# A graph network on one core: layer 2's input product y made by rows, with the data stationary and the weights moving

## The chip, the core and the metric

The kernel runs on one core of a Trainium2 chip. The metric is the device time of one execution in microseconds (us), the median of several runs. A profile of one execution gives the durations below; its times are counted from the start of its span. The engines are TensorE (PE: matmuls, with its weight loads listed apart as PEld), VectorE (DVE), ScalarE (ACT), GpSimd (POOL) and SyncE (SP), which here only issues DMAs. SBUF is the on-chip memory with 128 partitions; PSUM is the memory that TensorE writes its results to.

## The reference

Four graph layers run one after the other on 16 graphs of 1024 nodes with 128 features each; all of it in float32. Between layers the result is added to the input and normalised along the features. Layer 0 is a gated attention, layer 1 three graph convolutions with batch norm, layer 2 an attention with three gates, layer 3 three graph convolutions. The change lies where the end of layer 1 enters layer 2:

```python
h1 = _bn(jax.nn.relu(_sage(x, adj_d, Wr1, Wx1, b1, mf)), g1, be1)
h2 = _bn(jax.nn.relu(_sage(h1, adj_d, Wr2, Wx2, b2, mf)), g2, be2)
h3 = _bn(jax.nn.relu(_sage(h2, adj_d, Wr3, Wx3, b3, mf)), g3, be3)
xc = jnp.concatenate([h1, h2, h3], axis=-1) * mf[..., None]
return (xc @ Wl + bl) * mf[..., None]          # this is y
```

So y (1024 rows of 128 per graph) is the sum of three products of h1, h2, h3 with the three 128x128 blocks of Wl, plus a bias bl along the row, times a mask mf per row. It is then added to x, normalised (mean and variance along the features), and goes into layer 2. A batch below is one of the 16 graphs.

## The kernel before

The kernel has one code path for the general case and a fast one; the profile shows the fast one. Its stages follow each other: layer 0 (to about 740 us), the thinning of the adjacency for layer 1 (to about 1150 us), layer 1 (to about 1825 us), and layers 2 and 3 together (the rest). Each h_l is written to DRAM transposed, as 128 features x 1024 nodes, before batch norm. The batch norm, which is known only when all 16 batches are done, is a scale and an offset per feature (`bn_ab`). `take_norms` (L1220) folds it into layer 2's weights: the scale into the rows of Wl, the offset through a product with Wl into the bias.

Layers 2 and 3 work on one batch at a time in three generators: `before` (L1541: y, the addition to x, layer norm, x transposed, and the products hT and G), `attention` (L1574: eight blocks of 128 rows; each makes scores `pmm` on TensorE, a masked maximum `em` on VectorE at L1587, an exponential on ScalarE at L1591, a scaled `hs` on VectorE at L1598, and a product into `acc` on TensorE at L1601) and `after` (L1604: gates, layer norm, then layer 3: an ELU into `ehi` at L1505 to L1513, products with U at L1522 giving `zn`, `zhi`, `zlo`, and products with the adjacency at L1536). `in_turn` (L814) runs them interleaved: `before` of batches 0 and 1 first, then, for each batch b, `after` of b-1, `attention` of b and `before` of b+1. A scheduler of the framework turns this into one fixed order of instructions for each engine and places the waits. Each engine works through its order one after the other.

In `before`, y is made transposed: for each half of 512 nodes, three products with Wl stationary and hb (the transposed h_l) moving sum in PSUM; ScalarE copies the half into yT and adds the bias, which is a column there; four transposes on TensorE turn it back to rows, and VectorE multiplies them by the mask into yn (L1551). VectorE then adds yn to xn (L1554).

Helpers: `halves` (L747) gives two PSUM tiles of 512 columns, `turned` (L753) transposes eight blocks into them (L758), and `products` (L761) sums products into them (L765). The PSUM pool `ps_h` has two buffers, which all of these share. `normed` (L786) is the layer norm: statistics on VectorE (`ln_st`, `ln_mv`), a power on GpSimd (`ln_rstd`, L744), `ln_nb` on VectorE (L798), and eight ScalarE operations on xn (L800). The inputs of a batch come by SP's queue in `load` (L1229): A8, the three tiles hb0 to hb2 (one buffer each) and xn. `dB` (L1636) is a row of degrees for layer 3 from the same queue.

## Time and profile before

| what | value |
|---|---|
| median of 3 runs | 3009.3 us |
| lowest and highest of them | 3008.72 and 3012.13 us |
| the profiled run, timed | 3009.7 us |
| span of its profile | 3007.9 us |
| mean granted TensorE clock | 0.971 |
| y: products L765 with hb | 192 records, median 592 ns |
| y: transposes L758 of yT | 128 records, median 273 ns |
| y: ScalarE L1548, yT | 32, median 668 ns |
| y: VectorE L1551, yn | 32, median 681 ns |
| addition L1554 to xn, whole | 14, about 1220 ns |

A float32 product shows as two records each for the weight load and the matmul, a transpose as one. Lines of a timeline give the start, the length, the engine, the line, the operation, its output and inputs, their shapes and how many records are merged; a bracket at the end gives idle time of the engine before it and what ended it. The ends of matmuls are modelled, so that merged records overlap the next row; the starts are what to go by. The granted clock is a share of TensorE's full speed.

### The profile page before, as it was taken

How to read it: one execution, taken by the hardware profiler on the slowest of the kernel's cores; microseconds unless marked ns; L12 is line 12 of the kernel's file. 1: busy time of each engine (PE TensorE's matmuls, PEld its weight loads, DVE VectorE, ACT ScalarE, POOL GpSimd, SP SyncE). 2: the span in 40 equal slices, each digit the busy share in tenths (PEclk: the TensorE clock that was granted, in tenths of full speed). 3: DMA queues.
4: the chain of work that ended last, by engine and by line, in shares of the span. 5: the costliest groups of instructions: out<-in, count | busy, mean ns of one | idle time of the engine just before them, and what ended most of it. 6: DMA issues, size and time to landing. Idle time of an engine off the chain costs nothing.

```text
span 3007.9 us, 42998 instructions
## 1 busy us (share of the span) xinstructions
PE 2738.6 (91%) x15219; PEld 1719.6 (57%) x15282; DVE 2329.1 (77%) x5987; ACT 2028.3 (67%) x3475; POOL 324.1 (11%) x295
## 2 busy tenths in 40 slices
PE   7999999996999988999999987999999999999995
PEld 3444444443666566887788874455555555555554
DVE  6898899887999995776688785766777777777765
ACT  5777787774788877665555434766666676676763
POOL 0000000003000001211122231000010001000000
PEclk9999999998999999999999997999999999999998
DMA  4344444431000024223367692011111111111000
GB/s 157 133 161 153 135 140 161 148 126 36 2 2 2 2 102 143 99 99 127 127 234 250 227 342 84 36 56 58 63 69 61 64 70 66 56 57 57 22 15 23
DMA packets 124129, 297.98 MB, mean 99 GB/s; under 512 B 12672, under 2 KB 65664, under 8 KB 116736
## 3 DMA queue, kind: packets, MB, share of 16 engines
q1 hardware_dynamic: 103440, 211.65, 20.8%
q0 software_dynamic: 20464, 83.47, 7.4%
q8 instruction: 123, 2.02, 0.3%
q14 instruction: 102, 0.84, 0.1%
HBM read 211.04 MB, written 84.02 MB: 98 GB/s over the span
## 4 chain that ended last, share of the span: by engine, by line
PE 36%; DVE 23%; issue 21%; ACT 9%; DMA 6%; POOL 5%; SPq 0%; POOLq 0%; DVEq 0%; ACTq 0%
PE ph L1536 8%; PE acc L1293 6%; PE ph L765 5%; PE acc L1601 4%; DMA an<-in_adj 4%; PE pmm L723 3%; POOL ln_rstd L744 3%; DVE ln_st L793 3%; ACT xn L800 3%; PE ph L1397 3%; PE ph L758 3%; PE ph L1522 2%; DVE em L1587 2%; ACT em L969 2%; PE acc L976 2%
## 5 line engine op out<-in xcount | busy, mean ns | idle before, releaser
L723 PE MATMUL pmm<-G,hT 128*128 128x512 f32 x1024 | 505.9, 611 | 7.7 <-DVE mx L1587 7.2
L800 ACT ACTIVATE xn<-xn,ln_nb,ln_rstd 128x128 f32<-128x128 f32 x512 | 207.6, 481 | 115.2 <-DVE ln_nb L798 115.2
L723 PEld LDWEIGHTS pmm<-G,hT 128*128 128x128 f32 x1024 | 178.5, 193 | 175.5 <-issue 139.9
L976 PE MATMUL acc<-em,hs 128*128 128x512 f32 x512 | 243.3, 598 | 16.7 <-DVE hs L973 15.2
L1293 PE MATMUL acc<-a,lo 128*128 128x512 f32 x768 | 243.0, 400 | 15.2 <-DVE lo L1260 15.2
L744 POOL TENSOR_TENSOR ln_rstd<-ln_rstd,mhalf 128x8 f32<-128x8 f32 (+1 forms) x68 | 113.6, 1671 | 1329.1 <-DVE ln_rstd L741 608.8
L1601 PE MATMUL acc<-em,hs 128*128 128x512 f32 x512 | 249.3, 606 | 3.6 <-DVE hs L1598 1.9
L1293 PE MATMUL acc<-a,hi 128*128 128x512 f32 x768 | 244.1, 402 | 3.7 <-ACT hi L1259 3.5
L1140 ACT ACTIVATE q<-s,negc 128x512 f16<-128x512 f32 x256 | 170.5, 697 | 57.9 <-DVE negc L1119 22.3
L922 ACT ACTIVATE ab<-an 128x1024 bf16<-128x1024 f32 x128 | 134.5, 1052 | 105.9 <-DMA an<-in_adj 75.6
L1138 PE MATMUL s<-step,carry 128*128 128x384 bf16 (+3 forms) x1034 | 197.8, 302 | 7.5 <-DVE carry L1108 3.2
L1152 ACT ACTIVATE carry<-pc,negone 128x512 fp8e4<-128x512 f32 x256 | 166.8, 699 | 36.6 <-PE pc L1151 27.2
L965 DVE CUSTOM_DVE_ANT_0 em<-pmm,msk 128x1024 f32<-128x1024 f32 x128 | 155.9, 1218 | 30.0 <-PE acc L976 26.3
L1587 DVE CUSTOM_DVE_ANT_0 em<-pmm,msk 128x1024 f32<-128x1024 f32 x128 | 155.7, 1216 | 25.5 <-PE acc L1601 20.9
L1293 PEld LDWEIGHTS acc<-a,lo 128*128 128x128 f32 x768 | 143.9, 189 | 54.6 <-DVE lo L1260 21.2
L925 DVE SCALAR_TENSOR_TENSOR chk<-an 128x1024 fp8e4<-128x1024 f32 x128 | 156.4, 1222 | 14.8 <-DMA an<-in_adj 14.1
L1293 PEld LDWEIGHTS acc<-a,hi 128*128 128x128 f32 x768 | 142.9, 190 | 37.1 <-ACT hi L1259 4.0
L1582 ACT ACTIVATE msk<-A,nbig 128x1024 bf16<-128x1024 fp8e4 x128 | 145.8, 1140 | 26.7 <-DVE mx L1587 23.4
L930 DVE TENSOR_SCALAR carry<-pt 128x1024 fp8e4<-128x1024 bf16 x128 | 155.6, 1216 | 6.5 <-PE pt L929 6.5
L1397 PE MATMUL ph<-Wx,hT 128*128 128x128 f32 x768 | 152.3, 281 | 5.0 <-DVE l2WT L709 3.2
L969 ACT ACTIVATE em<-em,nmx 128x1024 f32<-128x1024 f32 x128 | 146.8, 1147 | 12.3 <-DVE nmx L967 11.9
L976 PEld LDWEIGHTS acc<-em,hs 128*128 128x128 f32 x512 | 90.7, 190 | 112.1 <-issue 86.8
(289 smaller groups left out, 6258.9 us busy)
## 6 DMA issues: line engine op xcount, KB each, us to landing
an<-in_adj SPq DMA_DIRECT2D x128, 512.0 KB, 4.1
adj_d<-carry POOLq DMA_DIRECT2D x16, 1024.0 KB, 4.9
A<-dil_d SPq DMA_DIRECT2D x16, 1024.0 KB, 6.8
rdeg<-rdeg_d SPq DMA_DIRECT2D x32, 512.0 KB, 4.3
ag_d<-ag POOLq DMA_DIRECT2D x32, 512.0 KB, 5.3
ag<-ag_d SPq DMA_DIRECT2D x32, 512.0 KB, 6.0
A<-adj_d SPq DMA_DIRECT2D x16, 1024.0 KB, 4.7
xn<-in_x SPq DMA_DIRECT2D x16, 512.0 KB, 4.0
```

The source lines that it names most:

```text
L723: nc.tensor.matmul(p[:, h * 512:(h + 1) * 512], lhsT, rhs[:, h * 512:(h + 1) * 512], start=True, stop=True)
L744: nc.gpsimd.tensor_tensor(r, r, mhalf[:, :n], op=OP.pow)
L800: nc.scalar.activation(r[:, k.start + i, :], r[:, k.start + i, :], AF.Identity, scale=rstd[:, i:i + 1], bias=nb[:, i:i + 1])
L969: nc.scalar.activation(em, em, AF.Exp, bias=nmx, accum_out=sm)
L976: nc.tensor.matmul(s.acc[:, c], hs, em[:, c], start=(jt == 0), stop=(jt == NT - 1))
L1138: nc.tensor.matmul(s[:, lo or 0:], y, twos if lo is None else step[:, :512 - lo], start=(j == 0), stop=(j == len(terms) - 1))
L1140: nc.scalar.activation(q[:, h * 512:(h + 1) * 512], s, AF.Abs, bias=st.negc[:, i:i + 1])
L1293: nc.tensor.matmul(acc, part[:, jt, :], pieces[h * NT // 2 + i][:, j, :], start=(jt == 0 and p == 0), stop=(jt == NT - 1 and p == 1))
L1397: nc.tensor.matmul(p[:, i * P:(i + 1) * P], x[:, j * P:(j + 1) * P], W, start=(n == 0), stop=(n == 1))
L1536: nc.tensor.matmul(p, part[:, jt, :], A[:, jt, c], start=(jt == 0 and i == 0), stop=(jt == NT - 1 and i == 1))
L1587: nc.vector.tensor_tensor_reduce(em, e, msk, 1.0, 0.0, op0=OP.add, op1=OP.max, accum_out=mx)
L1601: nc.tensor.matmul(s.acc[:, c], hs, em[:, c], start=(jt == 0), stop=(jt == NT - 1))
```

## The change

y is made by rows. For each of four blocks of 128 nodes in a half, the block of hb is the stationary operand and Wl moves: three products of 128 columns sum to 128 rows of y in PSUM. This makes 24 products a batch instead of 6, and no transposes and no yT. The bias is now a row, the same on all partitions (`blrow`), and VectorE adds it on the way out of PSUM; a second VectorE operation multiplies by the mask in place. `take_norms` makes the offset as a row too: the offset column of `bn_ab`, repeated 128 times, is stationary, and Wl moves.

```diff
-            self.blcol = column(wts, t["L1_gnn_bl"], "blcol")
+            self.blrow = row_bcast(wts, t["L1_gnn_bl"], P, "blrow")
...
-            pc = psum.tile([P, 1], F32, name="pc", tag="h")
+            pc = psum.tile([P, P], F32, name="pc", tag="h")
             for l in range(3):
-                nc.tensor.matmul(pc, self.Wl[:, l, :], bn_ab[l][:, 1:2], start=(l == 0), stop=(l == 2))
-            nc.vector.tensor_add(self.blcol, self.blcol, pc)
+                nc.tensor.matmul(pc, bn_ab[l][:, 1:2].to_broadcast([P, P]), self.Wl[:, l, :], start=(l == 0), stop=(l == 2))
+            nc.vector.tensor_add(self.blrow, self.blrow, pc)
...
-            yT = wide("yT")
-            for p, c in products(ps_h, *((Wl[:, l, :], s.hb[l]) for l in range(3))):
-                nc.scalar.activation(yT[:, c], p, AF.Identity, bias=blcol)
             yn = rows("yn", 2)
-            for p, c, k in turned(ps_h, yT):
-                nc.vector.tensor_mul(yn[:, k, :], tiles3(p), half_rows(mf[:, b * NT + k.start:b * NT + k.stop]))
+            for p, c, blocks in halves(ps_h):
+                for i, j in enumerate(blocks):
+                    for l in range(3):
+                        nc.tensor.matmul(p[:, i * P:(i + 1) * P], s.hb[l][:, j * P:(j + 1) * P], Wl[:, l, :],
+                                         start=(l == 0), stop=(l == 2))
+                k = slice(blocks[0], blocks[-1] + 1)
+                y = yn[:, k, :]
+                nc.vector.tensor_add(y, tiles3(p), blrow[:, None, :].to_broadcast([P, 4, P]))
+                nc.vector.tensor_mul(y, y, half_rows(mf[:, b * NT + k.start:b * NT + k.stop]))
```

Lines after the change are shifted: the new products are L1550, the addition L1554, the multiplication L1555, the addition to xn L1558; later lines are four higher.

## The prediction

> **What bounds the kernel now.** I read the page's busy shares first, then the two windows of the last stage that differ, then the order of instructions around the lines that change. The page says that no engine is idle enough to be ignored:
>
> ```profile
> PE 2738.6 (91%) x15219; PEld 1719.6 (57%) x15282; DVE 2329.1 (77%) x5987; ACT 2028.3 (67%) x3475; POOL 324.1 (11%) x295
> ```
>
> The change touches only the stage after 1828 us: a start-up of two batches (1828 to 1854 us), then one period per batch. The y products of batches 2 to 15 begin at 1903.73, 1974.81, 2046.41, 2117.43, 2188.04 ... 2825.20 us: 14 times, (2825.20 - 1903.73)/13 = 70.9 us apart. In the table by windows (PE, PEld, DVE, ACT, POOL, clock, DMA) TensorE is busy 92 to 97% there, VectorE 66 to 76%:
>
> ```profile
> 2000.00:2100.00 100.00, 93.08 (x366) 58.49 (x367) 66.66 (x194) 63.75 (x125) 6.83 (x4) 0.97 0.12 43
> 2200.00:2300.00 100.00, 91.89 (x341) 53.61 (x339) 72.71 (x234) 69.18 (x139) 10.11 (x6) 0.97 0.13 44
> ```
>
> Busy time alone would say "TensorE". The timelines of one period say more (start, length, then what ended the idle time in brackets):
>
> ```profile
> 2046.41 3.60 PE L765 MATMUL ph<-hb,Wl 128*128 128x512 f32 x8
> 2049.84 3.60 PE L1601 MATMUL acc<-em,hs 128*128 128x512 f32 x8
> 2053.27 1.88 PE L765 MATMUL ph<-hb,Wl 128*128 128x512 f32 x4
> 2054.99 0.60 PE L758 MATMUL ph<-identf,yT 128*128 128x128 f32 x4
> 2055.43 1.88 PE L1601 MATMUL acc<-em,hs 128*128 128x512 f32 x4
> 2057.15 0.60 PE L758 MATMUL ph<-identf,yT 128*128 128x128 f32 x4
> 2063.38 1.87 PE L758 MATMUL ph<-identf,xn 128*128 128x128 f32 x5 [2.20 <-ACT xn L800]
> ```
> ```profile
> 2051.76 1.23 DVE L1587 CUSTOM_DVE_ANT_0 em<-pmm,msk 128x1024 f32<-128x1024 f32 x1 [1.58 <-PE acc L1601]
> 2056.38 0.69 DVE L1551 TENSOR_TENSOR yn<-ph,mf 128x512 f32<-128x512 f32 x1
> 2062.63 0.17 DVE L798 SCALAR_TENSOR_TENSOR ln_nb<-ln_mv,ln_rstd 128x8 f32<-128x8 f32 x1 [1.55 <-POOL ln_rstd L744]
> ```
>
> The y work lies in the one part of the period where TensorE does idle: 2.20 us before the transposes of xn, and 2.01 us at 2073.00 (waiting for ehi). In that part the chain of waits runs on VectorE: em after the acc products, gating, layer norm, ELU. VectorE itself waits 1.58 us just before em. So a saving on TensorE counts only as far as it brings that em forward, or as other products move into the gaps.
>
> [...] the duration of a 128x128 f32 record (275 ns) is not its price. The timeline of L1397, the same form as the new products (data stationary, a weight matrix moving), shows the pace:
>
> ```profile
> 1600.94 0.39 PE L1397 MATMUL ph<-Wx,hT 128*128 128x128 f32 x2
> 1603.62 0.39 PE L1397 MATMUL ph<-Wx,hT 128*128 128x128 f32 x2
> ```
>
> Twelve products of two records in 2.68 us: 0.223 us a product, weight load included. [...] Here the granted clock was 0.50 from 1828 to 1834 us. [...] the power on GpSimd takes 2.62 us at 2059.98, beside the xn addition L1554, and 1.64 us at 2065.35. [...] the trace's 128x512 subtraction L1527 takes 686.
>
> **The change, part by part.** Removed per batch: six products of 128x512 (12 records at 3.43/8 = 0.43 us: 5.16 us), eight transposes (4 take 0.44 us: 0.88 us), two ScalarE evictions yT (0.668 us each). Added: 24 products at 0.223 us = 5.36 us (from above, 0.128 us a record, the pace that L1522's 16 records in 2.05 us show: 6.14), and two VectorE operations. VectorE before: two multiplications from PSUM, 0.68 us each. After: two additions from PSUM with a broadcast row (L1399, the same form, median 0.682 us) and two multiplications SBUF to SBUF (0.69 us). So TensorE -0.68 us (bound: +0.10), ScalarE -1.34, VectorE +1.37 per batch.
>
> Where that lies follows from the built order of the changed kernel, laid against the timeline above, with the start of the y products as zero. TensorE: 14 products (3.13), four acc products (3.44), ten products (2.23), two acc products (1.72): 10.5 us against 11.2 before. VectorE gets the first half's addition and multiplication between the hs scalings, before em. The first half is ready at 12 x 0.223 = 2.7 us, when VectorE comes free (about 3.0), so these two (1.3 us) fall into the 1.58 us in which it waited: no cost. Em can start 3.13 + 1.72 = 4.85 us after zero instead of 5.16: -0.31. The second half's addition and multiplication stand where the two old multiplications stood: no change. Its addition may wait up to 0.4 us for the second half (8.8 us); queued behind it are layer-norm statistics of the batch before, for which TensorE's xn transposes wait. Two further moves: one acc product (0.86 us) now lies between L1522 and L1536, where TensorE idled 0.44 us, so 0.42 net is gained; and y starts up to 0.46 us earlier, after half a product pmm instead of a whole one. Both bounds of one period: nothing gained if the VectorE chain decides, 0.31 + 0.42 + 0.46 = 1.2 us if all add up. I take 0.6, close to the saved TensorE time: 14 x 0.6 = 8.4 us.
>
> Start-up. The tiles hb0 to hb2 have one buffer, so batch 1's loads wait until batch 0's products have read them. Before, each layer's tile was free after its own two products:
>
> ```profile
> 1830.29 0.32 SPq L1235 DMA_DIRECT2D hb<-h0T_d  x1
> 1830.71 0.38 SPq L1636 DMA_DIRECT2D dB<-dinv_d  x1
> 1833.71 0.32 SPq L1235 DMA_DIRECT2D hb<-h1T_d  x1
> 1834.87 0.32 SPq L1235 DMA_DIRECT2D hb<-h2T_d  x1
> ```
> ```profile
> 1837.39 4.56 PE L765 MATMUL ph<-hb,Wl 128*128 128x512 f32 x10 [0.20 <-DVE yn L1551]
> 1843.72 1.64 PE L758 MATMUL ph<-identf,yT 128*128 128x128 f32 x8 [1.77 <-ACT yT L1548]
> ```
>
> After, the last block of rows reads all three. Two products run earlier; 22 remain from 1828.3: 25 of the 44 records at half clock (0.223 us) until 1834, 19 at 0.112: end 1836.1. The three loads are issued at about 1835.9, 1836.3 and 1836.7; with the 4.8 us to landing that this window's table of DMA issues gives for h2T, the third is there at 1841.5. TensorE idles 5.3 us, so I expect half clock for 3 to 6 us, and an end of the 24 products at 1848.3 to 1850. Add three VectorE operations (2.0): 1850.3 to 1852, against 1847.28 for the last xn addition before. The transposes and the products L765 of both batches stand behind this on TensorE. I take +4 us (from +1.2 at full clock to +5). The wait moves dB ahead of hb on SP's queue; dB waits for work finished by 1828, so nothing stands behind it.
>
> One-off terms: blrow's load is 64 KB written instead of 0.5 KB, with over 80 us to land; three products of 128 columns instead of one for the offset and an addition of 0.28 instead of 0.15 us, on the path: +0.2. Batch 0's hb2 load moves behind two loads on SP, some 5 us, with 36 us to spare. Sum: -8.4 + 4 = -4.4 (the 0.2 is in the 1828.3). Against the profiled span 3007.9 that gives 3003.5; that run was timed at 3009.7 and the median is 3009.3, so I carry the difference over: 3009.3 - 4.4 = 3004.9.
>
> **The rivals.**
> - *TensorE bounds all the way*: the whole 0.68 to 1.0 us per period is gained and the start-up costs 1.2: about -10 us, 2999. For it: TensorE 94% busy, and periods of different VectorE order before are within 1.1 us of each other (70.48 to 71.60). Against: TensorE's waits from 1850 to 2950 us sum to 70.6 us, 4.5 per period.
> - *The period is set by the VectorE chain*: the first half comes too late for the gap or the gap closes, but nothing is lost. Steady gain 0, start-up +4: 3013. For it: y lies wholly in the part with idle TensorE.
> - *VectorE becomes the bound*: the 1.37 us stand in its queue ahead of em and the statistics. It decides from the point at which VectorE comes to the first addition with under 1.3 us left before em. 14 x 1.37 + 4 = +23: 3032; a third of it, 3015.7, is already slower. For it: em and ln_st hold 5.9% and 5.4% of the chain of waits from 1850 to 2950 us. Against: the measured 1.58 us.
> - *The products don't pace as in L1397* but at 0.128 us a record: TensorE +0.10 per batch, about 3014.
>
> **How the numbers follow.** What a measurement of this kernel can tell from no change is 0.2%, 6 us. Forecast -4.4 us: 0.48 (of it 0.17 faster, 0.31 same). TensorE-bound: 0.25, faster. Chain-bound with nothing gained, slow pace with it: 0.12 (0.10 same, 0.02 slower). VectorE-bound: 0.15 (0.01 same, 0.14 slower). Sum: faster 0.42, same 0.42, slower 0.16. Range: the lower end is 1.2 x 14 = 16.8 less 4, 2996; the upper takes a third of the VectorE case, 3016. The forecast's own range is 2998 to 3010.
>
> **What would show it.** Right: L1550 at 0.223 us a product; no idle time before em of over 0.4 us; y starts 70.2 to 70.6 us apart; batch 1's products waiting for DMA at about 1841 and xT's products at about 1858 instead of 1854.19. Wrong: a period longer than 70.9 with VectorE idle no more than before, or a start-up without a DMA wait.

## The result and the profile after

The changed kernel takes 3022.7 us (median of 6 runs, 3016.9 to 3029.6) where the kernel before, on the same chip, takes 3010.1 (6 runs, 3006.6 to 3013.4): a ratio of 1.0042, with a 95% interval from 1.0026 to 1.0057. It is slower by 0.42%; the forecast was 0.15% faster. The profiled span grew from 3007.9 to 3021.0 us, by 13.1.

The y products of batch 2 now start at 1907.04 us instead of 1903.73 (+3.3, the start-up). From there to the last ones (2836.22) lie 13 periods of 71.48 us instead of 70.88 (+7.7): a steady loss of 0.6 us per period, where 0.6 us of gain were forecast. From the last y products to the end of the span it is 184.8 instead of 182.7 us (+2.1; this part was not taken apart). That is the whole 13.1.

The first part of the page after the change (busy time, share, instructions of each engine), and the two windows of the last stage:

```profile
PE 2741.9 (91%) x15730; PEld 1762.3 (58%) x15730; DVE 2348.1 (78%) x6019; ACT 2010.7 (67%) x3443; POOL 329.8 (11%) x295
```
```profile
2000.00:2100.00 100.00, 92.81 (x394) 57.96 (x393) 70.94 (x202) 67.42 (x133) 6.83 (x4) 0.98 0.12 43
2200.00:2300.00 100.00, 89.78 (x362) 53.90 (x362) 73.35 (x235) 66.81 (x135) 11.07 (x6) 0.97 0.17 58
```

In the two windows TensorE is a little less busy and VectorE a little more; over the whole run ScalarE is 17.6 us less busy. What the change does to the amount of work came out about as expected, and the time went the other way. The prediction's own sign of being wrong came true: a period longer than 70.9 us with VectorE idle no more than before. The timelines of one period show more. TensorE after the change (start, length, the rest as before):

```profile
2048.42 3.39 PE L1550 MATMUL ph<-Wl,hb 128*128 128x128 f32 x28 [0.29 <-DVE yn L1620]
2051.90 3.67 PE L1605 MATMUL acc<-em,hs 128*128 128x512 f32 x8
2055.40 2.39 PE L1550 MATMUL ph<-Wl,hb 128*128 128x128 f32 x20
2057.64 1.88 PE L1605 MATMUL acc<-em,hs 128*128 128x512 f32 x4
...
2064.83 2.01 PE L758 MATMUL ph<-identf,xn 128*128 128x128 f32 x5 [2.74 <-ACT xn L800]
2066.64 2.07 PE L1605 MATMUL acc<-em,hs 128*128 128x512 f32 x2
2068.50 0.85 PE L758 MATMUL ph<-identf,xn 128*128 128x128 f32 x3
2070.06 1.02 PE L765 MATMUL ph<-x3T,U 128*128 128x512 f32 x2
```

y takes less of TensorE, but TensorE idles 2.74 us before the transposes of xn in every period; in the kernel before it was 2.20 and 0.53 us in turn. Then something odd: the two acc records at 2066.64 take 1.86 us until the next row starts, where two such records elsewhere take 0.86. VectorE in the same period:

```profile
2051.74 0.67 DVE L1554 TENSOR_TENSOR yn<-ph,blrow 128x512 f32<-128x512 f32 x1
2052.52 0.68 DVE L1555 TENSOR_TENSOR yn<-yn,mf 128x512 f32<-128x512 f32 x1
2053.89 1.22 DVE L1591 CUSTOM_DVE_ANT_0 em<-pmm,msk 128x1024 f32<-128x1024 f32 x1
...
2060.53 0.66 DVE L1555 TENSOR_TENSOR yn<-yn,mf 128x512 f32<-128x512 f32 x1
2061.11 0.16 DVE L741 TENSOR_SCALAR ln_rstd<-ln_mv 128x8 f32<-128x8 f32 x1
2061.31 1.22 DVE L1558 TENSOR_TENSOR xn<-xn,yn 128x1024 f32<-128x1024 f32 x1
2064.08 0.17 DVE L798 SCALAR_TENSOR_TENSOR ln_nb<-ln_mv,ln_rstd 128x8 f32<-128x8 f32 x1 [1.55 <-POOL ln_rstd L744]
```

The first half's addition and multiplication fill the old wait ahead of em, which no longer waits. The second half's multiplication stands ahead of ln_rstd, and the addition to xn stands behind it with only a short operation between, in every period.

The kernel before has two kinds of period that take turns. In one, whose timelines the prediction shows, both old multiplications and the addition stand in the same places as here (2056.38, 2059.08 and 2059.86 us, with ln_rstd at 2059.66), and a second em stands ahead of them. In the other, 71 us later, one multiplication stands behind ln_rstd, and the addition comes only after ln_nb (VectorE before the change, in its order):

```profile
2128.68 0.66 DVE L1551 TENSOR_TENSOR yn<-ph,mf 128x512 f32<-128x512 f32 x1
2129.25 0.16 DVE L741 TENSOR_SCALAR ln_rstd<-ln_mv 128x8 f32<-128x8 f32 x1
2129.32 0.68 DVE L1551 TENSOR_TENSOR yn<-ph,mf 128x512 f32<-128x512 f32 x1
2131.26 0.17 DVE L798 SCALAR_TENSOR_TENSOR ln_nb<-ln_mv,ln_rstd 128x8 f32<-128x8 f32 x1 [1.25 <-POOL ln_rstd L744]
...
2131.47 1.22 DVE L1554 TENSOR_TENSOR xn<-xn,yn 128x1024 f32<-128x1024 f32 x1
```

The waits of TensorE from 1850 to 2960 us (line waited for, us in all, times, longest), before and after:

```profile
PE ph L1522 <- DVE ehi L1509: 25.8, 14, 2.6
PE ph L758 <- ACT xn L800: 22.4, 16, 3.2
```
```profile
PE ph L758 <- ACT xn L800: 39.5, 15, 3.4
PE ph L1522 <- DVE nmx L1593: 20.0, 13, 1.5
PE ph L1522 <- DVE ehi L1509: 8.4, 14, 3.0
```

The wait for xn grew by 17 us, which is more than the 0.68 us per period that y was to save. The start-up is as forecast: three loads issued together once batch 0's last block is done, a wait for DMA on TensorE, and xT's products at 1858.02 us instead of 1854.19:

```profile
1835.51 0.32 SPq L1235 DMA_DIRECT2D hb<-h0T_d  x1
1836.47 0.32 SPq L1235 DMA_DIRECT2D hb<-h2T_d  x1
```
```profile
1839.15 0.68 PE L1550 MATMUL ph<-Wl,hb 128*128 128x128 f32 x4 [3.23 <-DMA hb<-h0T_d]
1842.18 7.20 PE L1550 MATMUL ph<-Wl,hb 128*128 128x128 f32 x40 [0.66 <-DMA hb<-h2T_d]
1858.02 4.33 PE L765 MATMUL ph<-xT,l2WT 128*128 128x512 f32 x6
```

### The profile page after: what moved, and what is told of

The parts are those of the page before. It is cut to its first block, busy times and chain, and to the rows that moved or that the text cites. A ratio compares the mean times of both kernels' runs of the same rounds, so it can differ in the third digit from the quotient of the medians.

```text
span 3021.0 us, 43994 instructions
## 1 busy us (share of the span) xinstructions
PE 2741.9 (91%) x15730; PEld 1762.3 (58%) x15730; DVE 2348.1 (78%) x6019; ACT 2010.7 (67%) x3443; POOL 329.8 (11%) x295
## 4 chain that ended last, share of the span: by engine, by line
PE 34%; issue 21%; DVE 19%; ACT 15%; POOL 5%; DMA 5%; SPq 0%; POOLq 0%; ACTq 0%; DVEq 0%
PE ph L1536 8%; PE acc L1293 6%; ACT xn L800 5%; PE acc L1605 4%; POOL ln_rstd L744 3%; PE ph L765 3%; PE ph L758 3%; DMA an<-in_adj 3%; PE pmm L723 3%; PE ph L1397 3%; PE acc L976 3%; DVE ln_st L793 2%; ACT em L969 2%; ACT em L1595 2%; PE ph L1522 2%
## 5 line engine op out<-in xcount | busy, mean ns | idle before, releaser
L723 PE MATMUL pmm<-G,hT 128*128 128x512 f32 x1024 | 498.8, 605 | 2.8 <-DVE mx L1591 2.8
L1605 PE MATMUL acc<-em,hs 128*128 128x512 f32 x512 | 265.7, 635 | 3.2 <-ACT elo L1507 1.6
L976 PE MATMUL acc<-em,hs 128*128 128x512 f32 x512 | 243.3, 598 | 16.6 <-DVE hs L973 14.9
L1293 PE MATMUL acc<-a,lo 128*128 128x512 f32 x768 | 243.9, 402 | 15.1 <-DVE lo L1260 15.1
L1138 PE MATMUL s<-step,carry 128*128 128x512 bf16 (+2 forms) x1088 | 209.7, 305 | 4.1 <-DVE carry L1108 3.2
L1591 DVE CUSTOM_DVE_ANT_0 em<-pmm,msk 128x1024 f32<-128x1024 f32 x128 | 156.2, 1220 | 14.7 <-PE pmm L723 11.8
```

The lines of the kernel that those rows point to most:

```text
L723: nc.tensor.matmul(p[:, h * 512:(h + 1) * 512], lhsT, rhs[:, h * 512:(h + 1) * 512], start=True, stop=True)
L976: nc.tensor.matmul(s.acc[:, c], hs, em[:, c], start=(jt == 0), stop=(jt == NT - 1))
L1138: nc.tensor.matmul(s[:, lo or 0:], y, twos if lo is None else step[:, :512 - lo], start=(j == 0), stop=(j == len(terms) - 1))
L1293: nc.tensor.matmul(acc, part[:, jt, :], pieces[h * NT // 2 + i][:, j, :], start=(jt == 0 and p == 0), stop=(jt == NT - 1 and p == 1))
L1605: nc.tensor.matmul(s.acc[:, c], hs, em[:, c], start=(jt == 0), stop=(jt == NT - 1))
```

## The experiments

Positions in a period are counted from `gt` on VectorE (L1613 before, L1617 after), with which the chain of gating, layer norm and ELU starts: **nb** is the start of the next `ln_nb` after it. **Spacing** is the mean distance of the starts of the y products of batches 2 to 15. A **half-clock window** is a stretch of 3.413 us in which the granted clock is 0.50 (the fifth part shows it in the traces). They are counted in slices of 0.2 us from 1975 to 2825 us: the share of time at granted clock 0.50, times 850, by 3.413 us. Every group of runs has its own runs of the kernel before on its chip, so the ratios are compared, not the medians. A ratio comes from several executions; the other columns are those of the one execution that was profiled. "x/y" are alternating periods.

| run | ratio to before (95%) | spacing, us | nb, us after gt | half-clock windows in 12 periods |
|---|---|---|---|---|
| before | 1 | 70.88 | 14.8/17.6 | 12 |
| changed kernel | 1.0042 (1.0026 to 1.0057) | 71.48 | 16.6 | 12 |
| e1_old_start | 1.0019 (1.0010 to 1.0029) | 71.72 | 16.6 | 13 |
| e2_no_mask | 0.9965 (0.9953 to 0.9978) | 70.31 | 16.2 | 17 |
| e3_before_plus_mul | 0.9931 (0.9919 to 0.9943) | 69.42 | 14.8 | 6 |
| e4_scalar_evicts | 1.0006 (0.9996 to 1.0016) | 71.13 | 16.2 | 11 |
| f1_addition_behind | 0.9947 (0.9933 to 0.9962) | 69.91 | 15.7 | 6 |
| f2_before_add_behind | 1.0099 (1.0082 to 1.0116) | 73.41 | 16.6/15.4 | 18 |
| f4_mult_behind | 0.9985 (0.9976 to 0.9993) | 70.35 | 15.2 | 15 |
| f3_half_behind | 0.9963 (0.9949 to 0.9977) | 70.08 | 14.7 | 17 |
| h4_before_same_order | 0.9995 (0.9985 to 1.0006) | 70.82 | 15.1 | 9 |
| h4_after_same_order | 0.9948 (0.9934 to 0.9961) | 69.93 | 15.7 | 8 |
| g5_em_out_of_elu | 1.0117 (1.0102 to 1.0132) | 73.35 | 16.6 | 26 |
| c1_old_start_behind | 0.9924 (0.9911 to 0.9937) | 69.91 | 15.7 | 6 |
| d1_two_inputs_beside | 1.0026 (1.0013 to 1.0038) | 71.46 | 16.6 | 12 |
| d2_one_input_beside | 1.0034 (1.0021 to 1.0047) | 71.49 | 16.1 | 12 |
| k5_before_new_order | 0.9904 (0.9886 to 0.9921) | 68.58 | 14.8 | 1 |
| c2_diag_behind_zn | 1.0063 (1.0048 to 1.0077) | 72.66 | 15.7 | 6 |
| n2_keep_busy | 1.0033 (1.0022 to 1.0044) | 71.48 | 16.6 | 12 |
| n13_keep_busier | 1.0012 (1.0002 to 1.0023) | 71.09 | 16.6 | 8 |

An **order edge** below is an entry for the scheduler, "this instruction is issued behind that one on its engine". It computes nothing. It can move other instructions, though, on TensorE and ScalarE as well.

### First: start-up, occupancy, order

Theories for the steady loss: **occupancy** (1.37 us more on VectorE per batch stand in the chain), **order** (the addition to xn now stands behind ln_rstd in every period, and GpSimd's power beside it takes 2.62 us instead of 1.64 to 1.66; the text calls this longer power the lock), **ScalarE order** (msk took yT's place between the two tanhs).

e1_old_start:

```diff
+            if b < 2:
+                yT = wide("yT")
+                for p, c in products(ps_h, *((Wl[:, l, :], s.hb[l]) for l in range(3))):
+                    nc.scalar.activation(yT[:, c], p, AF.Identity, bias=l2.blcol)
...
+            else:
                 for p, c, blocks in halves(ps_h):
```

> The changed kernel, but batches 0 and 1 make y the old way (products, ScalarE eviction, eight transposes, one multiplication per half); batches 2 to 15 are as changed. Start-up theory (one buffer each of hb0 to hb2, so the last block of rows of batch 0 holds up all three loads of batch 1): the DMA wait in L765's old place goes back below 1 us, xT's products are at about 1854 instead of 1858 and the whole run is 3 to 4 us shorter than the changed kernel, about 3019 (ratio to before 1.003); the spacing of later y starts stays at 71.5 us. Rival (the later start is absorbed, because the first attention waits for something else): the same time as the changed kernel, about 3022.7 (1.004).

Measured: xT's products at 1854.24 us (1858.02 in the changed kernel); from the stage's first product to batch 2's y 75.8 us instead of 79.0 (before: 75.5). Spacing 71.72. **The start-up theory holds**: 3.2 us of the loss are the three single buffers. The 0.23% between the two ratios is more than 3.2 us, but the two intervals overlap.

e2_no_mask:

```diff
-                nc.vector.tensor_mul(y, y, half_rows(mf[:, b * NT + k.start:b * NT + k.stop]))
```

> The changed kernel without the multiplication of y by the mask (left out: the mask, which is all ones here), so VectorE has two additions from PSUM per batch and nothing more, as many operations as before. VectorE-occupancy theory (the 1.37 us more of VectorE per batch stands in the chain): the spacing falls from 71.5 to 70.9 or below, the run to 3007 to 3014. Order theory (the xn addition stands right behind ln_rstd in every period [...]): in this kernel's built order the xn addition stands ahead of ln_rstd, so the power should take 1.65 us in nearly every period, and the run gains too, by about 7 us. ScalarE-order theory (msk between the two tanhs, because yT is gone): no gain beyond 2 us, about 3021. The first two are told apart by the next run.

Measured: spacing 70.31, the power 1.65 us in every period. Both occupancy and order asked for a gain, so it tells against the ScalarE order alone.

e3_before_plus_mul (on the kernel before):

```diff
                 nc.vector.tensor_mul(yn[:, k, :], tiles3(p), half_rows(mf[:, b * NT + k.start:b * NT + k.stop]))
+                nc.vector.tensor_mul(yn[:, k, :], yn[:, k, :], half_rows(mf[:, b * NT + k.start:b * NT + k.stop]))
```

> The kernel before, with one more multiplication of y by the mask per half, SBUF to SBUF (the mask is applied twice), so that VectorE has the 1.37 us more per batch that the change adds, while TensorE, ScalarE and the start-up's loads are as before. VectorE-occupancy theory: slower than before by 0.5 to 1.3 us per period, 3017 to 3029. Order theory: the built order has the xn addition behind ln_nb or ahead of ln_rstd, so the power stays at 1.65 us in most periods, and the run is within 4 us of before, 3007 to 3014. ScalarE-order theory: no change, 3010.

Measured: **0.69% faster than before, with 1.37 us more work per batch on VectorE**. No theory had this. With the extra multiplications the addition to xn, em blocks and the addition of the diagonal stand in other places; ln_nb now comes at 14.8 us in every period, and half-clock windows are halved in number. The occupancy theory, in the form "more VectorE time is more time", has fallen.

e4_scalar_evicts:

```diff
-                nc.vector.tensor_add(y, tiles3(p), blrow[:, None, :].to_broadcast([P, 4, P]))
-                nc.vector.tensor_mul(y, y, half_rows(mf[:, b * NT + k.start:b * NT + k.stop]))
+                nc.scalar.activation(yT[:, c], p, AF.Identity, bias=half)
+                nc.vector.tensor_mul(y, tiles3(yT[:, c]), half_rows(mf[:, b * NT + k.start:b * NT + k.stop]))
```

> The changed kernel with the rows evicted by ScalarE (a constant is added in place of the bias row: the bias is left out) and only the multiplication by the mask on VectorE, from SBUF: TensorE has the new products, ScalarE and VectorE have as much as before. VectorE-occupancy theory: no more VectorE time than before and less TensorE time, so spacing 70.2 to 70.9, the run 3004 to 3014 (start-up loss of 4 us kept). Order theory: the built order has the xn addition right behind ln_rstd, so the power takes 2.6 us in most periods and the spacing stays above 71.2, the run at 3018 to 3024. ScalarE-order theory: ScalarE has an eviction in yT's place again, so the gain comes back, 3004 to 3014.

Measured: spacing 71.13, the power 2.62 us in every period. This fits no theory whole. The long power is what the order theory asked for, but the spacing lies between its 71.2 and the 70.9 of the others, and the ratio, 1.0006, is as the others asked. With ScalarE and VectorE loaded as before and TensorE less, the old spacing did not quite come back. So e4 decides nothing; e2 is what tells against the ScalarE order.

### Second: one order edge

f1_addition_behind (f2_before_add_behind is the same edit on the kernel before):

```diff
-            for k in spans(b < 2):
-                nc.vector.tensor_add(s.xn[:, k, :], s.xn[:, k, :], yn[:, k, :])
+            with behind(b):
+                for k in spans(b < 2):
+                    nc.vector.tensor_add(s.xn[:, k, :], s.xn[:, k, :], yn[:, k, :])
```

`behind(b)` is the edge: for batches 2 to 15, behind the ln_nb of the batch before. f4_mult_behind puts the second half's multiplication by the mask behind the same ln_nb too, f3_half_behind also its bias addition.

> The changed kernel with one edge for the order of VectorE's instructions: for batches 2 to 15 the addition of y to xn stands behind the layer norm's ln_nb of the batch before, so it no longer runs beside GpSimd's power; nothing is computed otherwise. Lock theory (the addition beside the power makes it 2.62 instead of 1.65 us in every period after the change, in every second one before it): the power takes 1.65 us everywhere, ln_nb comes 1.0 us earlier after gt (15.6 instead of 16.6 us), the spacing falls from 71.6 to about 70.6 us, the run to 3007 to 3011 (ratio to before 1.000, change to the changed kernel -0.4%). Occupancy theory (the two multiplications more on VectorE are the cause wherever the addition stands): no change, ratio 1.003 to 1.005.

> The kernel before with the same one edge (addition of y to xn behind ln_nb). Lock theory: the power falls from 2.62 to 1.65 us in the half of the periods that had the long one, so 6 or 7 times 1.0 us are gained: about 3003 where before is 3010, ratio 0.998. Occupancy theory: no change, ratio 1.000. If the order theory is wider than the lock (the run before with added multiplications had spacing 69.15 us, which the lock alone does not give: 70.9 - 0.5 = 70.4), the em blocks that move with it decide and the spacing may be anything from 69.2 to 71.

> As the changed kernel with the addition to xn behind ln_nb, and the second half's multiplication by the mask behind it too, so that this multiplication (0.66 us) no longer stands ahead of ln_rstd. Chain theory (what stands on VectorE ahead of ln_rstd delays the power, ln_nb, xn's normalisation and TensorE's transposes of it by its own length): ln_nb at gt+15.0 us, the spacing another 0.6 us shorter than with the addition alone, about 70.0 us; the run at 2999 to 3003, ratio 0.997. Occupancy theory: nothing is won by moving it, ratio as the changed kernel, 1.004.

> As the run before this, and the second half's bias addition from PSUM stands behind ln_nb as well, so that only the first half of the added VectorE work is ahead of ln_rstd. Chain theory: the power starts right after the statistics, ln_nb at gt+14.5 to 14.8 us, the spacing 69.3 to 69.8 us, the run at 2991 to 2998, ratio 0.994 to 0.996. Rival (the PSUM half stays occupied 4 us longer and TensorE's transposes of xn have to wait for one of the two ph buffers): the gain goes back, spacing 70.5 us or more, ratio 0.999 or more.

Measured: the one edge turns the changed kernel from 0.42% slower than before to 0.53% **faster** than before. Its power is 1.65 us everywhere and ln_nb comes 0.96 us earlier, as the lock theory said; but the spacing fell by 1.6 us, more than the lock, and the orders of VectorE and TensorE moved in other places too. The same edge makes the kernel before 1.0% **slower**: every second period takes 76 to 78 us, where 6 to 7 us were to be gained in all. And f4 and f3, in which ln_nb comes earlier still, are not faster than f1 (f4 is slower; f3's interval overlaps with f1's); in f3 TensorE's acc products wait for hs for 50.8 us in all. So ln_nb alone doesn't decide, and an edge is no local edit.

### Third: the change with the order held

h4_before_same_order and h4_after_same_order have the edge of f1 and one more:

```diff
-                nc.vector.tensor_tensor_reduce(em, e, msk, 1.0, 0.0, op0=OP.add, op1=OP.max, accum_out=mx)
+                with tc.issue_after(last_add[0]) if b >= 1 and jt == 4 else ExitStack():
+                    nc.vector.tensor_tensor_reduce(em, e, msk, 1.0, 0.0, op0=OP.add, op1=OP.max, accum_out=mx)
```

> The kernel before with two edges for VectorE's order in batches 2 to 15: the addition of y to xn behind ln_nb, and the em of the fifth block of attention behind that addition. The built VectorE order is then in every period that of those periods of the kernel before that have no long power. Order theory: the power is 1.65 us everywhere, ln_nb at gt+14.8 us, the spacing between 70.2 and 71.0 us as in those periods, ratio 0.996 to 1.001. Rival (a period's length is set by how the orders of TensorE and VectorE mesh, so that the same VectorE order in every period may be worth anything): spacing outside 70.0 to 71.2.

> The changed kernel with the same two edges, so that its VectorE order is that of the run before this one, apart from the change's own additions and multiplications: the change with the order held. Occupancy theory: ln_nb at gt+15.7 us (the second half's multiplication stands ahead of ln_rstd), spacing 0.6 to 1.2 us above the run before this, and with the start-up's 4 us this is +0.4 to +0.7% against it. Theory of the record (the first half's two operations lie in VectorE's wait and the saved TensorE time counts): spacing 0.3 to 0.9 us below the run before this, -0.3 to 0.0% against it with the start-up's loss.

> The changed kernel with one edge: the em of the sixth block of attention stands behind the second half of the first ELU instead of between its halves; the addition of y to xn still stands right behind ln_rstd, so the power stays at 2.62 us. This splits the gain of the run with the addition behind ln_nb (spacing 71.68 to 69.86 us) into its two parts, the lock and the em between the ELU halves. If the em counts: ehi's second half at gt+26.3 instead of 28.4 us and the spacing at 70.6 to 71.0 us, ratio 0.999 to 1.001. If only the lock counts: spacing as the changed kernel, 71.6 us, ratio 1.004.

> Candidate: batches 0 and 1 make y the old way, and for batches 2 to 15 (y by rows) the addition to xn stands behind ln_nb. If the two gains add up: 3.8 us (0.13%) less than the same edge without the old start, ratio 0.992 to 0.9945. If the later start was absorbed: 0.9947 as that run.

Measured: with VectorE's order held by the two edges, **the change shortens the spacing by 0.9 us** (70.82 to 69.93) and the run by 0.47% (0.9995 to 0.9948; 0.3% at most was expected), although ln_nb comes 0.6 us later and the start-up's loss is in it. Periods without a half-clock window take 69.84 to 69.87 us in the first and 69.43 to 69.47 in the second: 0.40 us of the gain are there without the clock. That is what the prediction's own theory asked for. TensorE's order was not held, though: ahead of the transposes of xn stand six records of pmm instead of four, and acc products moved as well; on VectorE one multiplication stands ahead of ln_rstd instead of behind it. The 0.9 us are the change together with this.

g5, meant to split f1's gain, moved one em out of the first ELU and left the lock:

```diff
+                with tc.issue_after(after_elu[0]) if b >= 2 and jt == 5 else ExitStack():
```

It is, with f2, the slowest run of all (TensorE's pmm waits for mx 37.8 us in all; two half-clock windows a period) and splits nothing. c1, f1 with the old start-up, gives 0.9924: the two gains add, within the intervals (batch 2's y 74.2 us after the stage's first product, against 78.9 in f1).

### Fourth: the lock alone, and the other order

d1 and d2 add to h4_after_same_order one VectorE operation between ln_rstd and ln_nb:

```diff
+                with tc.issue_after(gate_rs[0]):
+                    again = nc.vector.tensor_tensor(yn, yn, mf[:, b * NT:(b + 1) * NT][:, :, None].to_broadcast([P, NT, P]), op=OP.mult).ins
```

in d1, and in d2 `nc.vector.tensor_scalar(yn, yn, 1.0, None, op0=OP.mult).ins` in its place. k5_before_new_order gives the kernel before the VectorE order of the changed kernel:

```diff
+            if b >= 2:
+                tc.add_manual_dep(gate_nb[0], last_add[0].name, mybir.DependencyInfo(mybir.DependencyClass.NoSync, mybir.DependencyReason.DATA), reason="order")
...
+                with tc.issue_after(gate_nb[0]) if b >= 1 and jt == 4 else ExitStack():
```

The first edge puts ln_nb behind the addition to xn, the second the em of the fifth block behind ln_nb. c2 is c1 with the addition of the diagonal behind zn.

> The changed kernel with the order edges of the run 'change with the order held' and one more VectorE operation, which is issued between ln_rstd and ln_nb, where VectorE only waits for GpSimd's power: yn times the mask once more, 128x1024, both inputs from SBUF (the mask is applied twice). Its 1.2 us fit into the 1.64 us of the power. Lock theory: the power takes 2.6 us instead of 1.65, ln_nb comes at gt+16.6 instead of 15.7 us, and the spacing is about 1 us above that of the next run. Rival (the lock is a sign only, the em blocks decide): spacing within 0.2 us of the next run.

> As the run before this, with the added operation replaced by a multiplication of yn by the constant 1.0, 128x1024, one input from SBUF; the built order of VectorE is the same. Lock theory: the power stays at 1.65 us, ln_nb at gt+15.7 us, the spacing 69.6 to 70.2 us as in the run with the order held, ratio 0.994 to 0.996. Rival: as the run before this.

> The kernel before with edges that give VectorE the order of the changed kernel in every period: the addition of y to xn between ln_rstd and ln_nb, the em of the fifth block of attention behind ln_nb, which also brings one em between the two halves of the first ELU. With the two runs in which the order was held, this makes a table of two kernels by two orders. If the order explains the loss: spacing at or above the changed kernel's 71.6 us, ratio 1.002 to 1.010, although nothing is computed otherwise than before. If the change's own 1.37 us on VectorE explain it: spacing 70.9 us or less, ratio 1.000.

> Candidate: as the run with the old start-up and the addition behind ln_nb, and in every period the addition of the diagonal (1.22 us on VectorE, ahead of the ELU) stands behind the first zn. If the diagonal's 1.2 us lie in the chain from ln_nb to zn: ehi 0.8 to 1.2 us earlier, spacing 68.8 to 69.2 us, ratio 0.987 to 0.990. Rival (the copies of A, which need the diagonal, and the products with A become the later of the two): spacing as before or longer, ratio 0.992 to 0.998.

GpSimd's power in d1, and in d2 (start, length):

```profile
2060.77 2.62 POOL L746 TENSOR_TENSOR ln_rstd<-ln_rstd,mhalf 128x8 f32<-128x8 f32 x1 [12.89 <-DVE sm L1611]
```
```profile
2065.62 2.08 POOL L746 TENSOR_TENSOR ln_rstd<-ln_rstd,mhalf 128x8 f32<-128x8 f32 x1 [12.89 <-DVE sm L1611]
```

Measured: beside the operation with two inputs from SBUF (1.22 us) the power takes 2.62 us instead of 1.65, and beside the one with one input (0.69 us for the same 1024 columns) 2.08, which was not expected. ln_nb differs by 0.53 us between the two runs, the spacing by 0.03. **The lock is real and does not set the period here.** What it would cost elsewhere this pair can't tell. The 0.53 us still stand at the first ehi (25.42 us after gt in d1, 24.89 in d2, in periods with the same time from ln_nb to x3T's first product), but both runs keep step with the clock of the fifth part: d2's settled periods are 71.68 us, 21 of its windows, and d1 takes 84 windows for four. Both runs also lost the gain of h4_after_same_order: with the added operation one em stands behind the layer-norm statistics instead of ahead of them and acc products stand between TensorE's transposes of xn, and the spacing went from 69.93 to 71.5.

k5 is the surprise. With the edges that were to make it slower, the kernel before is 0.96% faster than before, and its time is the lowest of all. In its VectorE timeline ln_rstd is followed by y's second multiplication from PSUM, and only then by the addition to xn; GpSimd's line is below it, TensorE's last:

```profile
2055.75 0.66 DVE L1557 TENSOR_TENSOR yn<-ph,mf 128x512 f32<-128x512 f32 x1
2056.32 0.16 DVE L741 TENSOR_SCALAR ln_rstd<-ln_mv 128x8 f32<-128x8 f32 x1
2056.39 0.68 DVE L1557 TENSOR_TENSOR yn<-ph,mf 128x512 f32<-128x512 f32 x1
2057.12 1.22 DVE L1560 TENSOR_TENSOR xn<-xn,yn 128x1024 f32<-128x1024 f32 x1
2058.33 0.17 DVE L804 SCALAR_TENSOR_TENSOR ln_nb<-ln_mv,ln_rstd 128x8 f32<-128x8 f32 x1
```
```profile
2056.64 1.66 POOL L744 TENSOR_TENSOR ln_rstd<-ln_rstd,mhalf 128x8 f32<-128x8 f32 x1 [12.00 <-DVE ln_rstd L741]
```
```profile
2059.08 1.87 PE L758 MATMUL ph<-identf,xn 128*128 128x128 f32 x5 [0.53 <-ACT xn L806]
2060.88 1.12 PE L1610 MATMUL acc<-em,hs 128*128 128x512 f32 x2
2061.84 0.49 PE L758 MATMUL ph<-identf,xn 128*128 128x128 f32 x3
2063.03 1.02 PE L765 MATMUL ph<-x3T,U 128*128 128x512 f32 x2
```

The addition starts 0.48 us into the power, which takes 1.66 us. In the traces before and after the change the power takes 2.51 to 2.62 us in the 20 places where this addition is already running when it starts, and 1.64 to 1.66 in the 31 where an em is (1.22 us, pmm in PSUM and msk). TensorE's order is that of the changed kernel, apart from y itself. VectorE's is not quite: apart from the change's own operations, one multiplication stands behind ln_rstd in k5 and ahead of it in the changed kernel. Up to that place, k5 and the changed kernel are the change in a second order: 68.34 against 71.68 us (their settled periods), so **the changed kernel is 3.34 us longer here**. The timelines divide it: 1.84 us to ln_nb (0.88 of it until the power starts, at gt+13.1 and gt+13.98, and 0.97 for the lock), then from ln_nb to the first product with x3T 6.30 instead of 4.70 us in the settled periods, which is 1.60; the two are within 0.1 us of the whole. The 1.84 us hang on that one place: in k5 the multiplication is what runs when the power starts, and the power takes 1.66 us. The changed kernel with its multiplication there was not run. The 1.60 us are the slow stretch that begins with the odd pair of acc records above.

c2 is slower, more than even its rival expected: TensorE's products with A wait for ScalarE's copies of A (30.6 us in all), as that rival said.

### Fifth: the clock

The table by windows (PE, PEld, DVE, ACT, POOL, granted clock, DMA) of the changed kernel around the slow pair, and in slices of 0.2 us at the fall of the clock in three periods:

```profile
2067.00:2069.00 2.00, 2.00 (x5) 0.86 (x5) 1.32 (x4) 2.00 (x5) 1.44 (x1) 0.50 0.00 0
2069.00:2071.00 2.00, 2.00 (x7) 1.04 (x6) 2.00 (x7) 1.06 (x3) 0.00 (x0) 0.93 0.00 0
```
```profile
2065.80:2066.00 0.20, 0.14 (x2) 0.02 (x1) 0.20 (x5) 0.20 (x2) 0.00 (x0) 0.62 0.00 0
2137.40:2137.60 0.20, 0.20 (x1) 0.06 (x1) 0.20 (x5) 0.20 (x2) 0.00 (x0) 0.82 0.00 0
2209.20:2209.40 0.20, 0.16 (x1) 0.17 (x1) 0.20 (x4) 0.20 (x1) 0.00 (x0) 0.53 0.00 0
```

A slice at 0.62 is full speed for 24% of its 0.2 us, so the clock fell at 2065.85; in the same way at 2137.53 and 2209.21, 71.68 us apart. It rose again at 2069.26, 3.41 us later. The traces' own records of the granted clock give the same times. They hold two values, 1.00 and 0.50, and all their stretches, 56 before the change and 62 after, begin whole multiples of 3.4133 us apart, to 0.001 us; in the 12 periods each stretch at 0.50 is one such window long. 71.68 is 21 of them. The changed kernel's periods run 70.34, 71.04, 71.34, 71.52, 71.57, 71.62 and then stay at 71.64 to 71.69: they settle on 21 windows. In e1, whose orders in this part are the same, they come to it from the other side: the clock falls 19.1 us after y's start in the third period, then a little earlier in each (a period takes 71.76 to 71.79 us), down to 18.1. In the changed kernel it falls later in each period, from 16.8 us up to the same 18.1, and stays there. The kernel before keeps step in a longer pattern: from the fifth period on it repeats 70.49, 71.43, 70.78 and 70.63, in sum 283.33 us, which is 83 windows (283.31). The two kernels' settled periods are 21 and 20.75 windows, and the difference of a quarter window is 0.85 us. That the clock holds the period is read from this settling; no run tests it by itself.

n2_keep_busy and n13_keep_busier put TensorE work there (its result is overwritten by the transposes). n2:

```diff
             for p, c, blocks in halves(ps_h):
+                for _ in range(2 if blocks[0] == 0 else 0):
+                    nc.tensor.matmul(p, identf, s.xT[:, c], start=True, stop=True)
                 for i, k in enumerate(blocks):
                     nc.tensor.transpose(p[:, i * P:(i + 1) * P], s.xn[:, k, :], identf)
```

In n13 the moving operand is the second half of the next batch's yn, so that the products stand behind pmm, and this is added:

```diff
+                    if blocks[0] == 0 and i:
+                        nc.tensor.matmul(p[:, i * P:i * P + 128], identf, s.xT[:, k * P:k * P + 128], start=True, stop=True)
                     nc.tensor.transpose(p[:, i * P:(i + 1) * P], s.xn[:, k, :], identf)
```

> The changed kernel with two more products of 512 columns on TensorE per period (1.7 us; their result is overwritten by the transposes of xn), standing between y's products and the acc products, so that TensorE idles about 1.0 us instead of 2.74 before the transposes of xn; VectorE's built order is that of the changed kernel to the last instruction. Clock theory (in the changed kernel the granted clock is 0.50 for about 2 us right after this idle stretch, in every period, and the first product of x3T comes 6.2 us after ln_nb instead of 4.7): the clock stays at 1.0 there, x3T's first product 4.7 to 5.3 us after ln_nb, spacing 0.5 to 1.2 us below the changed kernel's 71.6, ratio 0.998 to 1.001, although TensorE has more to do. Rival (the idle stretch is a plain wait for xn and the clock has no part): spacing 71.6 us or more, ratio 1.004 or more.

> The changed kernel with TensorE kept busier where the granted clock falls: two products of 512 columns after the pmm products (1.7 us, in the 2.74 us of idle time) and one of 128 columns (0.22 us) ahead of each of the second to fourth transposes of xn, which come every 0.4 us; the results are overwritten by the transposes. VectorE's built order is that of the changed kernel to the last instruction, TensorE's that plus these products. Clock theory, in the form that the traces so far leave (the half clock begins and ends at multiples of 3.413 us, lasts one such window, comes once in a period after a window with little TensorE work, and holds the period at 21 windows, 71.68 us; one product less idle time was not enough): few or no half-clock windows here in batches 3 to 14 instead of one in each period, x3T's first product 4.7 to 5.3 us after ln_nb instead of 6.2, and the spacing leaves 71.68 us, to 70.2 to 71.2 us; ratio 0.998 to 1.001. Rival (the half clock is a sign and not a cause, or the load of TensorE doesn't set it): 12 windows in 12 periods, spacing 71.6 to 71.8 us, ratio 1.003 to 1.006.

TensorE in n2, and in n13, at the transposes of xn:

```profile
2063.55 2.74 PE L723 MATMUL pmm<-G,hT 128*128 128x512 f32 x6
2067.31 1.97 PE L1652 MATMUL ph<-identf,xn 128*128 128x128 f32 x5 [1.02 <-ACT xn L800]
2069.11 2.08 PE L1605 MATMUL acc<-em,hs 128*128 128x512 f32 x2
```
```profile
2056.38 1.88 PE L1653 MATMUL ph<-yn,identf 128*128 128x512 f32 x4
2059.29 0.33 PE L1657 MATMUL ph<-identf,xn 128*128 128x128 f32 x1 [1.02 <-ACT xn L800]
...
2061.09 1.13 PE L1608 MATMUL acc<-em,hs 128*128 128x512 f32 x2
2062.05 0.49 PE L1657 MATMUL ph<-identf,xn 128*128 128x128 f32 x3
```

The granted clock there (the sixth figure behind the length), in n2 and in n13:

```profile
2069.00:2071.00 2.00, 2.00 (x4) 0.75 (x4) 1.32 (x5) 2.00 (x5) 1.64 (x1) 0.50 0.00 0
```
```profile
2061.00:2063.00 2.00, 2.00 (x8) 1.15 (x8) 1.32 (x5) 2.00 (x5) 1.64 (x1) 1.00 0.00 0
```

n2: 1.7 us more TensorE work in every period, idle time 1.02 us instead of 2.74, and the half clock is still there, at the same place, in 12 of 12 periods. The spacing is the changed kernel's to the hundredth (71.48; settled periods 71.65 to 71.69). The clock theory as expected there (less idle time lifts the clock) failed. That the 1.7 us of work cost nothing is no sign of the 21 windows: they lie in idle time, and ln_nb and x3T's first product come as late after gt as in the changed kernel.

n13: with load between the transposes as well, the half clock at this place is gone, in 13 of 13 periods. The acc pair takes 0.96 us, x3T's first product comes 4.70 us after ln_nb, as in k5, and the first ehi 1.1 us earlier. Four periods without any half-clock window take 70.24 to 70.26 us (the first of the 13, which is not settled in any of the kernels, takes 68.82). In eight a half-clock window begins elsewhere, 21 windows apart, and they take 71.7 to 71.9. The instructions and their order are the same in all of them, so **the half clock is a cause**: a window costs n13 1.4 us or more. For the changed kernel the same 1.4 us is worked out from this, since its settled period is 71.68. The load that was added moved it out of some periods, not out of all, and the spacing (71.09) is just inside what was expected, the number of windows (8) is not "few".

The sum for the second order now closes: 68.34 (k5, without a half clock in its settled periods) and 1.84 to ln_nb make 70.18, against 70.25 measured in the clean periods of n13. From there to the changed kernel's 71.68 it is 1.43 us, against the 1.60 by which its x3T is later.

## Why the prediction was wrong

The step that failed is the bound of one period: nothing lost at worst, 1.2 us gained at best, 0.6 us taken. Measured is a loss of 0.6 us per period.

**Right.** The pace of the new products: 20 records in 2.24 us, 0.112 us a record or 0.223 a product (the first 28 take 3.48 until acc starts, 0.35 more than that pace; this was not taken apart). The start-up: +4 forecast, +3.8 us at xT's products, +3.3 at the y products of batch 2, by the mechanism that was named, and taken back by e1. The half clock behind the wait for DMA, an estimate of 3 to 6 us, lasted 6.83: the granted clock is 0.50 from 1840.57 to 1847.40 us. The first half's two operations in VectorE's wait: em starts at gt+6.43 us with and without them (k5 and the changed kernel), with no idle time left ahead of it. But em was also to come 0.31 us forward, and against k5 it did not: VectorE itself is now busy until then.

**Half right: "The second half's addition and multiplication stand where the two old multiplications stood: no change."** It is so in the kind of period that the sum was laid against. In the other kind, every second period of the kernel before, one of the two stood behind ln_rstd, and the power started at gt+13.1 us; now it starts 0.88 us later.

**Wrong: the lock was read and not priced.** The text read the power's 2.62 us beside the addition to xn, but the sum has no term for it, though the built order of the changed kernel has the addition behind ln_rstd in every period instead of every second one. It is 0.97 us to ln_nb in each further period. Together: ln_nb came 14.8 and 17.6 us after gt in turn, 16.2 on average, and now comes at 16.6 in every period. d1 and d2 show that such a shift of ln_nb need not reach the period.

**Wrong: the step "Both bounds of one period: nothing gained ... 1.2 us if all add up. I take 0.6".** It put the loss of a period at zero or better, from one of the two kinds of period. Both of the points above were visible in the other kind and make the lower bound negative. And the bound took a period for a sum of waits and work. What TensorE saved, and more, became idle time before the transposes of xn, and in every period the clock halved for 3.41 us from there; in n13, with more load there, this half clock is gone. A half clock was counted for the start-up alone. How much of the 0.6 us is the clock and how much the order stays open, since the kernel before has as many half-clock windows.

**Of the rivals** none is the cause. "VectorE becomes the bound" is nearest in time (3015.7 for a third of it, 3032 for the whole), but its point, less than 1.3 us left before the first addition, was not reached: the first addition was free. Its third is also summed wrongly: 3015.7 is a third of the 14 x 1.37 us without the start-up's 4; with them it is 3019.7, and the range would have ended there, still below the measured 3022.7. e3 shows that VectorE time by itself isn't the bound.

**Of the tests named**, the two on products and em held and the start-up's held. The spacing, "70.2 to 70.6", did not hold; 70.25 is what n13 takes in the periods without the half clock. That does not save the forecast: the kernel before has 12 half-clock windows in 12 periods too, keeps step with 83 of the clock's windows in four periods, and what it would take without them in its own order was not run.

**What is settled and what is open.** Settled: the loss of 0.6 us per period isn't a fixed price of the change's work. It is worth -0.9 us in one order, with TensorE's order moved beside it, and +3.3 in another, in which one multiplication stands elsewhere; and one edge on VectorE turns +0.42% into -0.53%. Open: what the change is worth with every engine's order held; which of the instructions that move with an edge makes f2 lose 1% or k5 gain 1%; and a rule for where half-clock windows begin. Their number doesn't rank the kernels: e2 and f3 have 17 of them and are faster than before.

The lowest time of the study is that of k5_before_new_order, the computation before with two order edges: 0.9904 (0.9886 to 0.9921). With y by rows it is c1_old_start_behind, at 0.9924 (0.9911 to 0.9937), the two intervals overlapping. Both are faster than the kernel before and the changed one.

## What to carry to other kernels

When a change moves a fixed order of instructions, the move can be worth more than the work: here the same work took from 68.3 to over 73 us per period. Hold the order with edges in both kernels, in more than one order, before judging the change; and put a price on each place where the built order of the new kernel differs from any kind of period of the old one, here a multiplication and an addition around ln_rstd.

A steady period that settles on one number to the hundredth, in kernels of different order, may be held by something with a beat of its own: here 71.68 us, 21 times the 3.413 us of the granted clock. An experiment with added work tells of this only if the work doesn't lie in idle time. Look at the granted clock in slices shorter than a microsecond.

## What the runs showed of the hardware that was not expected

- The half clock begins and ends at whole multiples of 3.413 us, to 0.001 us in the traces before and after the change, and a repeating program can settle in step with it: 21 windows, 71.68 us, in the changed kernel, in n2, and in d2, whose order is another.
- In the window ahead of it TensorE is partly busy. In the changed kernel it was busy 0.90 of the 3.41 us ahead of the fall at 2065.85, in the kernel before 2.60 ahead of the one at 2134.54. In n2 TensorE idled 1.02 us in that window, and otherwise had 0.8 us of pmm and five transposes at 0.4 us. In n13 three products of 128 columns between the transposes, and the two larger ones moved behind pmm, took the half clock at this place away.
- The lock between VectorE and GpSimd: beside the addition to xn, and in d1 beside another operation with two SBUF inputs (1.22 us, begun 0.12 us before), the power takes 2.62 us instead of 1.65, 0.97 more where 1.10 of the operation were left. Beside one with a single SBUF input (0.69 us, d2) it takes 2.08, and 1.66 when the addition starts 0.48 us later (k5). In this last case the addition ran its usual 1.22 us beside a power that had started first. What makes the power longer was not shown.
